# A two-layer 5x5 convolution: row combinations in unused columns, on ScalarE with adding transfers, and reflections on GpSimd

## The chip, the cores and the metric

The kernel runs on one core of a Trainium2 chip. The metric is the device time of one execution in microseconds (us). The kernel before takes 1879.63 us, the median of three runs (1878.62 to 1879.75).

## The reference

The input x has 8 images of 32 channels and 252x252 points, in float32. Two layers follow each other, and both compute the same thing with weights of their own:

```python
    # --- layer 0 (conv_preact) ---
    x = x + _L0_conv_ref(_gn(x), L0_conv_weight)
    # --- layer 1 (conv_preact) ---
    x = x + _L1_conv_ref(_gn(x), L1_conv_weight)
```

`_gn` is a group norm without scale and shift: 16 groups of 2 channels, with mean and variance over a group's whole image. The convolution is 5x5, 32 channels to 32, with two reflected points at each border; the reference writes it with Fourier transforms.

## The kernel before

**Layout.** An image is split by the parity of its columns and rows into four phases of 126x126. With 32 channels each, the phases fill the 128 partitions, and the 5x5 convolution becomes a 3x3 one from 128 to 128 channels. A *chunk* (b, l, c) is the piece c of 8 of image b in layer l (0 or 1); it has 16 rows of each phase, in 4 groups of 4.

**Arithmetic.** Rows are done by a short-convolution scheme with six points: six combinations of input rows, times six weight matrices, give four output rows. The combinations are built by VectorE (DVE) from two intermediates: `v` (16 rows: a row plus or minus the row two above it, `row_pairs`, L567 and L583) and `u` (2 times 4 rows: four times one row plus or minus the row two below it, `row_quads` and `last_rows`, L576, L577, L584). `point2` (L592) and `point1` (L602) are made from `u`; `point4` (L596), `point3` (L599) and `points05` (L609) from `v`. Along a row there are three taps, hence three matmuls for each point, accumulated in PSUM. For the two outer points many chunks are done "by columns" instead: DVE makes sums and differences along the row (`columns`, L618 to L628), and TensorE (PE) does 8 products of half the width (L707) instead of 6 full ones; four of these 8 read `sdiff` and go into the PSUM tile `extra`, and between the first two and the last two of them ScalarE (ACT) must halve a result (`seed_columns`, L711). The norm is folded into weights and biases, and the residual is added into the weights.

**Layer 1's v by transfers.** For nearly every chunk of layer 1, `v` isn't made by DVE: `row_sums` copies the rows of y by a transfer from GpSimd's queue (L557) into a tile with one buffer, and two adding transfers (L559, L560) add the rows two further down. L557 waits for the last reader of the tile's previous content (L609), L559 for the landing of L557.

**Buffers.** x's chunks lie in `xs`, 16 rows of 256 columns, in two buffers. A layer-0 chunk reads the even columns (0:256:2) alone. Most chunks are loaded once (`once`): partitions 0 to 63 get their image columns at odd and even places, `borders` (GpSimd, L148 to L154) makes the reflected columns, and `even_columns` (ACT, L159) copies the odd columns of partitions 0 to 63 into the even ones of partitions 64 to 127. In the tile pool `vpool` the names `v`, `va` and `u12` have one buffer each. Layer 0's results y stay in SBUF; `reflect` (ACT, L869 to L872) makes their four border columns, and rows in the first and last chunk.

**Order of the work.** The order is written out by hand. Every step is put in a table with a due time by `at`; the table is sorted by due time, and each engine executes its instructions in that order. After the first eight chunks, layer-0 chunks of image b+1 alternate with layer-1 chunks of image b. `begin(i)` is the planned start of the i-th chunk's matmuls. With two chunks by columns a layer-0 and a layer-1 chunk together take 27.2 in planned time, which is called a *pair* here. Around a layer-0 chunk planned at 0 and the layer-1 chunk at 13.6, ACT's order is: outer results of layer 0 (L785) at 0.05, seeds of PSUM (L729, L731) at 2.6 and 5.1, evacuations (L737, L744), `reflect` 7.8, `seed_columns` 9.3, small `even_columns` 9.35, the statistics of the next image (L235, L241) 9.8, squares (L860) 12.2, outer results of layer 1 (L785, or L773 where it isn't done by columns) at 13.65, interleaving for the output (L925), the seeds of the layer-1 chunk (L729, L731) at 16.2 and 18.7, its `seed_columns` 22.9. GpSimd's order is: small `borders` 5.5, `row_sums` L557 at 15.05, large `borders` 17.6, L559 and L560 at 22.0. SyncE's queue carries the loads of x (L143), the pieces for the statistics (L254) and the stores (L910).

Of the kernel before, what the change touches and what calls it, by code (L numbers as in the profile page):

```python
# [42 lines left out]
F32 = mybir.dt.float32  # L43
BF16 = mybir.dt.bfloat16
AF = mybir.ActivationFunctionType
ALU = mybir.AluOpType
# [3 lines left out]
P = 128  # L50
# [6 lines left out]
def tile_conv_preact_x2(ctx: ExitStack, tc: tile.TileContext, x: bass.AP, w0: bass.AP, w1: bass.AP, out: bass.AP):  # L57
# [34 lines left out]
    def at(t: float, fn, *args, **kw):  # L92
        table.append((t, len(table), fn, args, kw))
# [67 lines left out]
    def once(b: int, c: int) -> bool:  # L161

        return c != NCH - 1 and (c != 1 if b > 1 else c != 3 if b else True)

    def copied_late(b: int, c: int) -> bool:

        return once(b, c) and (b > 1 or (b == 1 and c > 3))

    def parts(b: int, c: int):

        if once(b, c):
            return ((0, 10), (10, 6)) if (b, c) == (0, 0) else ((0, 2), (2, 14))
        return ((0, ROWS),) + (((ROWS, 2),) if c == NCH - 1 else ())
# [363 lines left out]
    def transform(t0: float, t1: float, b: int, l: int, c: int, free: float = -100.0, now=(0, 0, 0)):  # L537

        wi = WIN[l]
        got = {}  # L540
        sent = l == 1 and (b, c) != (0, 0)

        def source():
            if l == 0:
                nxt = xs[b, c + 1] if c + 1 < NCH else xtail[b]
                return xs[b, c][:, :, 0:256:2], nxt[:, :, 0:256:2]
            return ytile[b, c], ytile[b, c + 1] if c + 1 < NCH else ytail[b]

        def row_sums(add: bool):

            t, nxt = source()
            if not add:

                i = max(order.index((b, l, c)) - order.index((B - 2, 1, NCH - 2)), 0)
                got["v"] = vpool.tile([P, ROWS, wi], F32, tag=("va", "v")[i % 2], name=f"v_{b}_{l}_{c}")
                got["vt"] = got["v"].rearrange("p (t i) w -> p t i w", i=4)
                G.dma_start(got["v"], t)  # L557
            else:
                G.dma_start(got["v"][:, 0 : ROWS - 2], t[:, 2:ROWS], accum_op=ALU.add)  # L559
                G.dma_start(got["v"][:, ROWS - 2 : ROWS], nxt[:, 0:2], accum_op=ALU.add)  # L560

        def row_pairs(j0: int = 0, j1: int = NT):
            if j0 == 0:
                got["v"] = vpool.tile([P, ROWS, wi], F32, tag="v", name=f"v_{b}_{l}_{c}")
            v, (t, nxt) = got["v"], source()
            r0, r1 = 4 * j0, min(4 * j1, ROWS - 2)
            (V.tensor_add if l else V.tensor_sub)(v[:, r0:r1], t[:, r0 + 2 : r1 + 2], t[:, r0:r1])  # L567
            got["vt"] = v.rearrange("p (t i) w -> p t i w", i=4)

        def row_quads(j0: int = 0, j1: int = NT):  # L570
            if j0 == 0:
                got["u"] = vpool.tile([P, 2, NT, wi], F32, tag="u12", name=f"u12_{b}_{l}_{c}")
            u1, u2, (t, nxt) = got["u"][:, 0], got["u"][:, 1], source()
            r0, k1 = 4 * j0, min(j1, NT - 1)
            f = 4.0 if l else -4.0
            stt(u1[:, j0:j1], t[:, r0 + 1 : 4 * j1 : 4], f, t[:, r0 + 3 : 4 * j1 : 4], ALU.mult, ALU.add)  # L576
            stt(u2[:, j0:k1], t[:, r0 + 2 : 4 * k1 : 4], f, t[:, r0 + 4 : 4 * k1 + 1 : 4], ALU.mult, ALU.add)  # L577

        def last_rows():

            u2, (t, nxt) = got["u"][:, 1], source()
            if not sent:
                (V.tensor_add if l else V.tensor_sub)(got["v"][:, ROWS - 2 : ROWS], nxt[:, 0:2], t[:, ROWS - 2 : ROWS])  # L583
            stt(u2[:, NT - 1], t[:, ROWS - 2], 4.0 if l else -4.0, nxt[:, 0], ALU.mult, ALU.add)  # L584

        def point2(j0: int = 0, j1: int = NT):
            if j0 == 0:
                t = tpool.tile([P, 2, NT, wi], F32, tag="t24", bufs=1, name=f"t24_{b}_{l}_{c}")
                if not fixed:
                    fixed.append(vpool.tile([P, 2, NT, WMAX], F32, tag="t13", name="t13"))  # L590
                ts[b, l, c] = {0: t, 1: fixed[0][:, :, :, 0:wi]}
            V.tensor_sub(ts[b, l, c][0][:, 0, j0:j1], got["u"][:, 1, j0:j1], got["u"][:, 0, j0:j1])  # L592

        def point4(j0: int = 0, j1: int = NT):
            vt = got["vt"][:, j0:j1]
            stt(ts[b, l, c][0][:, 1, j0:j1], vt[:, :, 1], -2.0, vt[:, :, 2], ALU.mult, ALU.add)  # L596

        def point3():
            stt(ts[b, l, c][1][:, 1], got["vt"][:, :, 1], 2.0, got["vt"][:, :, 2], ALU.mult, ALU.add)  # L599

        def point1():
            stt(ts[b, l, c][1][:, 0], got["u"][:, 1], norm[b, l][1][:, 1:2], got["u"][:, 0], ALU.add, ALU.add)  # L602

        def points05():
            if by_columns(b, l, c):
                t = vpool.tile([P, NT, 2, wi], F32, tag="u12", name=f"t05_{b}_{l}_{c}")
            else:
                t = tpool.tile([P, NT, 2, wi], F32, tag="t05", name=f"t05_{b}_{l}_{c}")
            stt(t, got["vt"][:, :, 0:2], 4.0 if l else -4.0, got["vt"][:, :, 2:4], ALU.mult, ALU.add)  # L609
            ts[b, l, c][2] = t  # L610

        def columns():

            t, (m, mo) = ts[b, l, c][2], evens_odds(l)
            sd = vpool.tile([P, 2, NT, 2, m], F32, tag="sdiff", name=f"sdiff_{b}_{l}_{c}")
            d = tpool.tile([P, NT, 2, 2, m], F32, tag="t05", name=f"d05_{b}_{l}_{c}")
            odd, even = t[:, :, :, 1 : 2 * m : 2], t[:, :, :, 2 : 2 * m + 1 : 2]
            V.tensor_add(sd[:, 0], odd, even)  # L618
            V.tensor_sub(sd[:, 1], even, odd)
            if m == mo:  # L620
                f = "p t e (m a) -> p (t e) a m"
                V.tensor_sub(
                    d.rearrange("p t e a m -> p (t e) a m"),
                    t[:, :, :, 0 : 2 * m].rearrange(f, a=2), t[:, :, :, 2 : 2 * m + 2].rearrange(f, a=2),
                )
            else:
                V.tensor_sub(d[:, :, :, 0], t[:, :, :, 0 : 2 * m : 2], t[:, :, :, 2 : 2 * m + 1 : 2])
                V.tensor_sub(d[:, :, :, 1, 0:mo], odd[:, :, :, 0:mo], t[:, :, :, 3 : 2 * mo + 2 : 2])  # L628
            ts[b, l, c][2] = d, sd

        if (b, l, c) == order[0]:
            at(t0 - 33.3, row_quads, 0, 2)
            at(t0 - 31, point2, 0, 2)
            for fn in (row_pairs, point4):
                at(t0, fn, 0, 2)
            at(t0 + 0.2, row_quads, 2, 4)
            at(t0 + 0.2, row_pairs, 2, 4)
            at(t0 + 0.2, last_rows)
            at(t0 + 0.2, point2, 2, 4)
            at(t0 + 0.2, point4, 2, 4)  # L640
            at(t0 + 4.9, point1)
            at(t0 + 5.5, point3)
            at(t0 + 6.2, points05)
        else:
            if sent:
                two = begin(order.index((b, l, c)) - 2)
                at(two + 1.45, row_sums, False)
                at(two + 8.4, row_sums, True)
            else:
                at(t0, row_pairs)  # L650
            for dt, fn in ((2, row_quads), (3.2, last_rows), (3.6, point2)):
                at(t0 + dt, fn)
            at(max(t0 + 4.2, free + 9.45) if sent else t0 + 4.2, point4)
            at(max(t0 + 5.5, free + 7.8), point1)
            at(max(t0 + 5.6, free + (11.1 if by_columns(*now) else 10.25)), point3)
            at(t1, points05)
            if by_columns(b, l, c):
                at(t1 + 1.5, columns)
# [184 lines left out]
    def keep(t1: float, t2, b: int, c: int, got):  # L843
# [17 lines left out]

        def reflect():
            lo, hi = (1 if c == 0 else 0), (ROWS - 1 if c == NCH - 1 else ROWS)
            y, copy, r = got["y"], A.copy, slice(lo, hi)

            def negated(dst, src):
                A.activation(dst, src, AF.Copy, scale=-1.0)
# [109 lines left out]
    def begin(i: int) -> float:  # L977

        return sum(10.2 + (own + [0.0])[j] + (late[j - 1] if j else 0.0) for j in range(i))
# [56 lines left out]
    for i, (b, l, c) in enumerate(order):  # L1036
# [11 lines left out]
        if i + 1 < len(order):  # L1048
# [3 lines left out]
            if nl == 0 and 2 < k < len(inputs):  # L1052
                kb, kc = inputs[k]
                for part in parts(kb, kc):
                    if copied_late(kb, kc):
                        at(t0 + 9.5, load, kb, kc, *part)
                        at(begin(i + 2) + 4.0 if part[0] else t1 + 5.5, borders, kb, kc, *part)
                        at(begin(i + 3) + 4.0 if part[0] else t1 + 9.35, even_columns, kb, kc, *part)
                        continue
# [77 lines left out]
```

## Time and profile before

| | before |
|---|---|
| median of 3 runs | 1879.63 us |
| the profiled execution: its own time | 1879.27 us |
| its span, first to last instruction | 1877.5 us |
| granted TensorE clock, mean | 0.994 |
| 16 DMA engines' busy share, 400 to 1600 us | 0.81 |
| packets, bytes on GpSimd's DMA queue | 27600, 134.20 MB (29.3% of the 16 engines' span) |
| packets, bytes on SyncE's DMA queue | 178832, 230.73 MB (49.8%) |

Busy times are sums over the span of one profiled execution; the program's own time is 1.8 us longer than the span. A row of instructions gives count, busy time and mean duration; a row of waits gives the total, the count and the longest wait in us.

### The profile page before, as it was taken

The numbers are of one execution on the slowest core, as the hardware profiler recorded it, in microseconds if no ns is written. First come the engines' busy times: TensorE is split into PE (matmuls) and PEld (weight loads), VectorE is DVE, ScalarE is ACT, GpSimd is POOL, SyncE is SP. The second block draws the span as 40 slices with busy tenths as digits, with TensorE's granted clock in tenths as the row PEclk, the third lists the DMA queues.
The fourth block names the chain that finished last, engine by engine and source line by source line (L and its number), as shares of the span: only waits on it lengthen the run. The fifth ranks groups of instructions, "written<-read, shape, count | busy, mean of one in ns | idle before, by whom it ended". The sixth has DMA issues, their size and how long they took to land.

```text
span 1877.5 us, 20381 instructions
## 1 busy us (share of the span) xinstructions
PE 1839.2 (98%) x5194; PEld 966.0 (51%) x5194; DVE 1731.2 (92%) x3030; ACT 1493.8 (80%) x2781; POOL 396.2 (21%) x855
## 2 busy tenths in 40 slices
PE   5999999999999999999999999999999999999998
PEld 4444455545555555555555455554555555555455
DVE  7988799999999999999999899999999999997796
ACT  5886788878887888888898798987898876765575
POOL 4543111131112211122111311113111141110211
PEclk8999999999999999999999999999999999999999
DMA  9877578878888877987878967888878866775785
GB/s 275 203 179 180 151 209 199 210 194 202 217 202 219 194 209 192 221 223 173 220 193 206 235 175 205 205 204 204 212 202 198 214 165 140 179 174 148 195 212 125
DMA packets 207110, 369.07 MB, mean 197 GB/s; under 512 B 19088, under 2 KB 173968, under 8 KB 196752
## 3 DMA queue, kind: packets, MB, share of 16 engines
q1 hardware_dynamic: 178832, 230.73, 49.8%
q0 software_dynamic: 27600, 134.20, 29.3%
q10 hardware_dynamic: 560, 2.83, 0.4%
q8 instruction: 41, 0.67, 0.2%
q14 instruction: 77, 0.63, 0.1%
HBM read 167.15 MB, written 67.39 MB: 125 GB/s over the span
## 4 chain that ended last, share of the span: by engine, by line
PE 80%; DVE 7%; DMA 6%; ACT 3%; issue 3%; SPq 0%; POOL 0%; DVEq 0%; ACTq 0%; POOLq 0%
PE m L685 28%; PE pairs L685 28%; PE sums L707 7%; PE extra L707 6%; PE sums L685 6%; PE extra L685 4%; DMA v<-y 2%; DMA st<-in_x_dram 1%; DMA v<-ytail 1%; DMA xs<-in_x_dram 1%; ACT o L925 1%; DVE sd L748 1%; DVE t L609 1%; DMA wraw<-in_L_conv_weight_dram 1%; DMA out_dram<-o 0%
## 5 line engine op out<-in xcount | busy, mean ns | idle before, releaser
L685 PE MATMUL pairs<-t,u 128*128 128x504 f32 (+2 forms) x1548 | 692.9, 586 | 5.4 <-ACT pairs L729 3.3
L685 PE MATMUL m<-t,u 128*128 128x508 f32 (+3 forms) x1560 | 674.8, 581 | 3.4 <-DVE u L526 1.9
L685 PEld LDWEIGHTS m<-t,u 128*128 128x128 f32 x1560 | 294.2, 189 | 317.1 <-issue 297.0
L685 PEld LDWEIGHTS pairs<-t,u 128*128 128x128 f32 x1548 | 290.2, 189 | 320.1 <-issue 289.1
L925 ACT COPY o<-y 64x508 f32<-64x508 f32 x496 | 327.5, 660 | 8.6
L748 DVE SCALAR_TENSOR_TENSOR sd<-sd,pairs 128x504 f32<-128x504 f32 (+2 forms) x258 | 164.2, 671 | 19.5 <-PE pairs L685 15.2
L707 PEld LDWEIGHTS extra<-sdiff,wc 128*128 128x128 f32 x680 | 125.9, 189 | 98.1 <-issue 47.8
L707 PE MATMUL extra<-sdiff,wc 128*128 128x252 f32 (+3 forms) x680 | 173.0, 376 | 3.4 <-ACT extra L711 2.3
L860 ACT ACTIVATE junk<-y,negk 128x1008 bf16<-128x1008 f32 (+1 forms) x144 | 147.4, 1024 | 31.1 <-PE extra L707 14.5
L557 POOL DMA_DIRECT2D v<-y x63 | 35.7, 567 | 622.7 <-DVE t L609 608.4
L737 ACT COPY sd<-m 128x504 f32<-128x504 f32 (+2 forms) x258 | 136.9, 581 | 33.3 <-DVE sums L794 28.1
L609 DVE SCALAR_TENSOR_TENSOR t<-v 128x1024 f32<-128x1024 f32 (+1 forms) x128 | 157.7, 1232 | 5.4 <-PE sums L685 5.4
L707 PE MATMUL sums<-d,u 128*128 128x252 f32 (+3 forms) x680 | 157.4, 374 | 0.0
L707 PEld LDWEIGHTS sums<-d,u 128*128 128x128 f32 x680 | 127.6, 189 | 24.9 <-issue 9.0
L685 PE MATMUL sums<-t,u 128*128 128x508 f32 (+5 forms) x312 | 133.6, 577 | 0.0
L567 DVE TENSOR_TENSOR v<-xs 128x1792 f32<-128x1792 f32 (+1 forms) x65 | 130.2, 2003 | 1.2
L241 ACT ACTIVATE st<-st,negk 128x1134 f32<-128x1134 f32 x98 | 121.7, 1242 | 3.2
L559 POOL DMA_DIRECT2D v<-y x63 | 54.3, 862 | 329.1 <-DMA v<-y 329.1
L159 ACT COPY xs<-xs 64x1792 f32<-64x1792 f32 (+2 forms) x97 | 109.3, 1129 | 13.4 <-POOL xs L151 11.1
L729 ACT ACTIVATE pairs<-m,means 128x504 f32<-128x504 f32 (+1 forms) x129 | 84.2, 653 | 44.5 <-PE m L685 36.0
L785 ACT ACTIVATE y<-sums 128x504 f32<-128x504 f32 (+1 forms) x158 | 94.5, 634 | 28.3 <-PE sums L707 19.2
L235 ACT ACTIVATE st<-st 128x1134 f32<-128x1134 f32 x98 | 112.5, 1148 | 5.0 <-DMA st<-in_x_dram 3.2
(174 smaller groups left out, 2529.7 us busy)
## 6 DMA issues: line engine op xcount, KB each, us to landing
v<-y POOLq DMA_DIRECT2D x63, 1032.0 KB, 6.1
st<-in_x_dram SPq DMA_DIRECT2D x111, 567.0 KB, 6.1
out_dram<-o SPq DMA_DIRECT2D x480, 126.0 KB, 5.9
v<-y POOLq DMA_DIRECT2D x63, 903.0 KB, 7.7
xs<-in_x_dram SPq DMA_DIRECT2D x96, 441.0 KB, 8.4
xs<-in_x_dram SPq DMA_DIRECT2D x44, 504.0 KB, 12.0
u<-ud SPq DMA_DIRECT2D x15, 1152.0 KB, 6.0
xs<-in_x_dram SPq DMA_DIRECT2D x16, 472.5 KB, 9.3
```

The source lines that it names most:

```text
L159: copy(t[64:128, :, 0:256:2], t[0:64, :, 1:256:2])
L235: A.activation(junk, src, AF.Identity, accum_out=acc[:, 0, i : i + 1])
L241: A.activation(junk, src, AF.Square, bias=negk, accum_out=acc[:, 1, i : i + 1])
L567: (V.tensor_add if l else V.tensor_sub)(v[:, r0:r1], t[:, r0 + 2 : r1 + 2], t[:, r0:r1])
L609: stt(t, got["vt"][:, :, 0:2], 4.0 if l else -4.0, got["vt"][:, :, 2:4], ALU.mult, ALU.add)
L685: T.matmul(dst, u[:, k, 2 - i, :], rhs[:, j0 + i0 : j0 + i1, i : i + wo], start=(i == 0 and not add), stop=(i == 2), skip_group_check=add,)
L707: T.matmul(dst[:, 0, use], w, rhs[:, use], start=(i == 2), stop=True, skip_group_check=(i != 2))
L737: A.copy(got["sd"][:, 1 + e], m24[e][:, 0:n])
L748: stt(d, d, -2.0, pairs13[e][:, 0:n], ALU.mult, ALU.add)
L785: A.activation(y, src, AF.Copy, scale=1.0 - 2 * i, **total(3 * i))
L860: A.activation(dst, src, AF.Square, bias=negk, scale=1.0 if i else -1.0, accum_out=acc[:, 1, at_ : at_ + 1])
L925: copy(got["o", h][halves[s], 0:m, cp::2], got["y"][halves[cp], r : r + m, :])
```

## The change

Layer 0's v is written into the odd columns of its own `xs` buffer, for images 2 to 7 and for chunks 4 to 7 of image 1. That keeps the buffer in use until `points05` has read v, so for the chunks that take such a buffer over (`deferred`) the load, the borders and the even columns get later due times, and all of them are loaded in two parts, of 2 and 14 rows.

For the layer-1 chunks behind chunk (0, 4) that follow a layer-0 chunk in the order (`sent_u`, 50 of them), `row_quads` and `last_rows` leave DVE. ACT writes four times the two inner rows of each group into the tile `v` (`four_times`), and three adding transfers from GpSimd's queue add the outer rows (`outer_rows`).

In chunks 1 to 6 `reflect` copies by GpSimd instead of ACT.

```diff
+    def among_columns(b: int, c: int) -> bool:
+        return b > 1 or (b == 1 and c > 3)
+    def deferred(b: int, c: int) -> bool:
+        i = inputs.index((b, c))
+        return i > 1 and among_columns(*inputs[i - 2])
     def parts(b: int, c: int):
+        if deferred(b, c):
+            return ((0, 2), (2, 14)) + (((ROWS, 2),) if c == NCH - 1 else ())
...
+        sent_u = l == 1 and (b, c) > (0, 4) and order[order.index((b, l, c)) - 1][1] == 0
...
+        def four_times():
+            got["u"] = vpool.tile([P, 2, NT, wi], F32, tag="v", name=f"ua_{b}_{l}_{c}")
+            src = source()[0].rearrange("p (t i) w -> p i t w", i=4)
+            A.activation(got["u"], src[:, 1:3], AF.Copy, scale=4.0)
+        def outer_rows():
+            t, nxt = source()
+            u1, u2 = got["u"][:, 0], got["u"][:, 1]
+            G.dma_start(u1, t[:, 3:ROWS:4], accum_op=ALU.add)
+            G.dma_start(u2[:, 0 : NT - 1], t[:, 4:ROWS:4], accum_op=ALU.add)
+            G.dma_start(u2[:, NT - 1], nxt[:, 0], accum_op=ALU.add)
         def row_pairs(j0: int = 0, j1: int = NT):
-            if j0 == 0:
+            if l == 0 and among_columns(b, c):
+                got["v"] = xs[b, c][:, :, 1:256:2]
+            elif j0 == 0:
                 got["v"] = vpool.tile([P, ROWS, wi], F32, tag="v", name=f"v_{b}_{l}_{c}")
...
                 at(two + 8.4, row_sums, True)
+                if sent_u:
+                    at(begin(order.index((b, l, c)) - 3) + 13.0, four_times)
+                    at(two + 1.4, outer_rows)
             else:
                 at(t0, row_pairs)
-            for dt, fn in ((2, row_quads), (3.2, last_rows), (3.6, point2)):
-                at(t0 + dt, fn)
+            for dt, fn in ((2, row_quads), (3.2, last_rows)):
+                if not sent_u:
+                    at(t0 + dt, fn)
+            at(t0 + 3.6, point2)
...
-            y, copy, r = got["y"], A.copy, slice(lo, hi)
+            y, copy, r = got["y"], A.copy if c in (0, NCH - 1) else G.tensor_copy, slice(lo, hi)
...
+                    if deferred(kb, kc):
+                        at(t1 + 6.0, load, kb, kc, *part)
+                        at(begin(i + 2) + 10.0 if part[0] else t1 + 11.0, borders, kb, kc, *part)
+                        if once(kb, kc):
+                            at(begin(i + 3) + 4.0 if part[0] else t1 + 12.6, even_columns, kb, kc, *part)
+                        continue
```

In the planned time of a pair (as above) the new places are: on ACT, `reflect` gone from 7.8 in chunks 1 to 6, small `even_columns` from 9.35 to 12.6, `four_times` at 13.0; on GpSimd, `reflect` at 7.8, small `borders` 11.0, `outer_rows` at 15.0 ahead of L557 at 15.05, large `borders` 23.6, behind L559 and L560; on SyncE's queue the load of x at 6.0, which before stood at 23.1 of the pair before.

## The prediction

> **What bounds the kernel now.** I read the engines' busy times first, then PE's waits, then one pair of chunks in order of time. The page's first part and the stretch from 400 to 1600 us (PE, weight loads, DVE, ACT, POOL, clock, DMA share):
>
> ```profile
> PE 1839.2 (98%) x5194; PEld 966.0 (51%) x5194; DVE 1731.2 (92%) x3030; ACT 1493.8 (80%) x2781; POOL 396.2 (21%) x855
> ...
> 400.00:1600.00 1200.00, 1198.10 (x3383) 630.16 (x3382) 1150.95 (x1978) 1011.54 (x1896) 230.30 (x502) 1.00 0.81 200
> ```
>
> TensorE (PE) idles 1.9 us in these 1200; the other 36 lie at the start, around 180 to 200 us and at the end, where the change touches little. The change removes no matmul, so it can hardly gain: what is left is the few waits of PE on its helpers.
>
> ```profile
> PE extra L707 <- ACT extra L711: 2.3, 8, 0.8
> PE extra L707 <- DVE sdiff L619: 0.5, 2, 0.3
> ```
>
> The danger is the reverse: an engine beside PE that gets late. In the pair at 1128 to 1155 us, ACT runs without a pause from L711 of the layer-0 chunk to L711 of the layer-1 chunk (start, duration):
>
> ```profile
> 1137.44 0.57 ACT L711 ACTIVATE extra<-extra 128x504 f32<-128x504 f32 x1 [0.37 <-PE extra L707]
> ...
> 1142.13 1.15 ACT L785 ACTIVATE y<-sums 128x512 f32<-128x512 f32 x2
> 1143.32 1.34 ACT L925 COPY o<-y 64x508 f32<-64x508 f32 x2
> 1144.68 0.66 ACT L729 ACTIVATE pairs<-m,means 128x508 f32<-128x508 f32 x1
> 1145.36 1.33 ACT L925 COPY o<-y 64x508 f32<-64x508 f32 x2
> 1146.81 0.57 ACT L731 COPY pairs<-m 128x508 f32<-128x508 f32 x1
> ...
> 1151.54 0.58 ACT L711 ACTIVATE extra<-extra 128x512 f32<-128x512 f32 x1
> ```
>
> PE's view of the same time:
>
> ```profile
> 1146.61 3.57 PE L685 MATMUL pairs<-t,u 128*128 128x508 f32 x8
> ...
> 1152.58 1.02 PE L707 MATMUL extra<-sdiff,wc 128*128 128x256 f32 x4
> ```
>
> L729 ends at 1145.34, 1.27 us before PE needs it (1146.61). L711 ends at 1152.12, 0.46 us before PE's second `extra` group.
>
> [...]L235's 1134 elements take 1148 ns[...].[...] L148's 64x4 copy taking 0.18 us at one place and 1.00 us at another[...].
>
> **The change part by part.**
>
> *Row combinations of layer 1.* DVE loses L576 (698 ns), L577 (557) and L584 (290): 1.55 us for each of 50 chunks, 77 us in all. DVE isn't the bound, so the worth is slack: DVE-made waits of PE vanish (0.5 us), and ACT's waits for DVE before L737 (28.1 us, 32 times) shrink, which shortens a few of ACT's late L711. Bounds 0 to -4 us; I take -2.
>
> ACT gains `four_times`, 1032 elements: [...]by the trace's L235 scaled 1.04[...]. It stands just ahead of L785 or L773 of the layer-1 chunk two places earlier. Where that is L773, ACT waits there for PE (70.9 us, 24 times, 3 us each) and swallows it: chunks 1, 5 and 7. Where it is L785 nothing absorbs it. L729 would end at 1146.3, still 0.3 early; L731 would start at 1147.8 instead of 1146.81, where it had waited for PE; L711 would end at 1153.0 to 1153.1, PE needing it at 1152.58 less some 0.05: **0.55 us late**. This holds where two by-columns chunks of layer 1 follow each other, chunks 2 and 3 of five images (image 6 has no statistics beside it): 10 x 0.55 = 5.5. At the change of image L729 has only 0.2 to 0.3 us of slack in the trace before some chunks (seeds at about 1089 and 1102 us): 0.4 an image, 2 in all. Together **+7.5 us**.
>
> The two places of ACT's small copy (L159, 0.43 us) lie in the same unbroken run, so moving it costs nothing; if the run had a gap between them, 0.43.
>
> *Reflections.* ACT loses 4 copies of 0.22 to 0.23 us in 48 chunks: 43 us. But they stand before L711 of layer 0, which waits for PE anyway (0.37 us in the row above); without them it waits 1.3. In an engine that runs in order the saving can't be carried behind that wait: 0 on PE's path. GpSimd gains 192 copies, 0.18 us (L148's shortest, as above) to 1 us[...], in stretches where it waits 6 to 13 us: 0.[...]
>
> *Adding transfers.* The rows are 516 bytes, so u takes 1024 packets. The trace's packet records have medians of 104 ns for an adding packet of 1032 bytes and 565 ns for 7224, a line that gives 66 ns at 516: 1024 x 66 / 16 = 4.2 us of all engines, against 0.19 x 27.2 = 5.2 us that a pair leaves free. It fits, but barely, by this count (which counts packets twice when two queues overlap). GpSimd must issue three more transfers: 0.55 us each by L557 (128 packets) if that doesn't grow with packets, up to 4.4 us for all if it does. They go ahead of L557, whose chain is this (GpSimd, then the reader of v on DVE):
>
> ```profile
> 1144.27 0.56 POOL L557 DMA_DIRECT2D v<-y  x1 [13.02 <-DVE t L609]
> ...
> 1151.27 0.87 POOL L559 DMA_DIRECT2D v<-y  x1 [5.93 <-DMA v<-y]
> 1151.82 1.23 POOL L560 DMA_DIRECT2D v<-y  x1
> ```
>
> `four_times` would end at about 1143.2, 1 us before L557 starts, so L557's data move 4.2 - 0.8 = 3.4 to 5.1 us later; elsewhere 1.4 to 4. v, landed at 1151.82 + 8.5 = 1160.3, is read at 1166.20 (L596), some 1164.7 with DVE's saving. So it mostly fits; where v is late already (L596 waits 17.6 us in 7 places), x's load, which no longer lies beside L559, gives about as much back. Bounds -1 to +10; I take +1.
>
> *v in x's columns.* DVE writes it at a stride of two. L793 does that already, at 675 ns against 688 for L792; reading at a stride costs nothing either (L576: 695 from xs, 698 from y). 0.
>
> *The later loads.* x is held until L609, about 3 us into the layer-0 chunk, and loaded at 6.0; the transfers land after 8 to 12 us (12.0 for the 504 KB ones). The small part (31.5 KB, 2.7 us) is wanted at 11, the large at 23.6. SyncE gains some 52 small issues of about 1 us, in a queue with gaps of several us: 0. The large `borders` now stand behind L559 and L560 and so behind the wait for L557's landing; ACT's L159 behind it has 5 to 10 us after L559 before. Less 2 us for issue and copies, less the 1.4 to 5.1 us from above, it keeps -0.5 to 2.6 us, and L731 behind it has 1.8 more: 0, bound +5.
>
> **Sum.** -2 + 7.5 + 1 + 0 = +6.5 on the profiled 1879.27 (span 1877.5 and 1.8 around it): 1885.8. That execution lies 0.4 us under the median of 1879.63. I forecast **1886**, +0.34%.
>
> **Rivals.** (0.2% is 3.8 us, about what a measurement of this kernel can tell from no change.)
>
> (a) *ACT late for L711*, as summed: 1882 to 1892, likeliest 1886. Chance 0.47.
>
> (b) *Absorbed*: not slower. ACT's insertion is paid by DVE's slack: L737 stops waiting for the sums (0.9 us a time), so L711 is ready where it was late before, and PE's waits on `extra` fall as the new ones come. It decides if the insertion costs under 0.5 us on the run from L711 to L711, the slack measured above; then the new stalls are 0 and the gains of 2 us stay: 1878 to 1881. For: the slack is 0.46, the insertion only twice that. Against: that run has no gap. Chance 0.30.
>
> (c) *Transfers late*: `outer_rows` holds GpSimd and the queue, L557 lands late, DVE waits at L596 and ACT at L159. It decides when L557 moves over 5 us. Then 1 us for each of 30 to 50 chunks, and more with full DMA engines: 1893 to 1930, centre 1905. Against: 4.2 us of packets and the slack shown. Chance 0.18.
>
> (d) *Faster*: DVE's slack removes most of PE's small waits and nothing new comes: 1874, about all that PE's rate between 200 and 1700 us leaves. Chance 0.05.
>
> Faster by over 0.2%: (d), 0.05. Within: (b) and a little of (a), 0.32. Slower: 0.63. The range leaves out about half of (c) and most of (d): 1877 to 1902.
>
> **What would show it.** PE's waits for L711 should rise from 2.3 us to about 8, at the layer-1 chunks 2 and 3; DVE's busy time fall by about 77, ACT's rise by about 8 (50 x 1.04 less 43); the new rows of `outer_rows` show the issue time, L559's wait for L557 should grow from 329 us, and L596's wait stay under 40. I am wrong if PE waits on DVE's L596 or L592, if L159 waits long for GpSimd, or if L711's waits don't grow.

## The result, and the profile after

| | before | after |
|---|---|---|
| median of the runs | 1879.69 us (4 runs) | 1946.74 us (1944.1 to 1949.28, 4 runs) |
| ratio, 95% interval | | 1.0359 [1.0343, 1.0376] |
| span of the profiled execution | 1877.5 us | 1943.6 us |
| granted TensorE clock, mean | 0.994 | 0.984 |

The kernel is 67 us slower, ten times the forecast of 6.5 us and outside the range of 1877 to 1902. Lines of the kernel after are up to 33 higher than before: L557, L559 and L560 became L570, L572 and L573; L596 became L624, L711 became L744, L731 became L764, L757 became L790. New are L579 (`four_times`) and L584 to L586 (`outer_rows`).

The page's first part and the stretch from 400 to 1600 us, as shown of before:

```profile
PE 1862.6 (96%) x5194; PEld 971.7 (50%) x5194; DVE 1662.2 (86%) x2880; ACT 1508.3 (78%) x2639; POOL 630.1 (32%) x1236
...
400.00:1600.00 1200.00, 1160.96 (x3229) 605.45 (x3228) 1039.79 (x1771) 988.31 (x1734) 390.89 (x763) 0.99 0.96 212
```

DVE lost 69 us of work and the DMA engines' share rose from 0.81 to 0.96, both close to what was expected. But PE, idle for 1.9 us of the 1200 before, is idle for 39. Its waits (total, times, longest in us):

```profile
PE extra L740 <- DVE sdiff L647: 21.9, 17, 3.1
PE pairs L718 <- ACT pairs L764: 18.9, 8, 2.8
...
PE extra L740 <- ACT extra L744: 6.1, 16, 0.8
PE m L357 <- DVE mv L347: 4.1, 6, 0.9
```

The third row is the wait that was predicted (8 us, 6.1 came). The first two are larger and longer. Most of their time comes in pairs, one of each a few us apart, at seven places of the program, five of them where the last layer-1 chunk of an image meets the next image. The trace of that place at the end of layer 1 of image 1, engine by engine. GpSimd (start, duration; in brackets the idle time before):

```profile
622.08 1.31 POOL L584 DMA_DIRECT2D ua<-y  x1
622.89 1.80 POOL L585 DMA_DIRECT2D ua<-y  x1
623.64 1.96 POOL L586 DMA_DIRECT2D ua<-y  x1
624.99 1.18 POOL L570 DMA_DIRECT2D v<-y  x1
...
637.73 0.85 POOL L572 DMA_DIRECT2D v<-y  x1 [11.56 <-DMA v<-y]
638.28 1.17 POOL L573 DMA_DIRECT2D v<-y  x1
```

DVE:

```profile
636.85 1.27 DVE L781 SCALAR_TENSOR_TENSOR sd<-sd,pairs 128x508 f32<-128x508 f32 x2
644.26 0.69 DVE L790 SCALAR_TENSOR_TENSOR y<-pairs,sd 128x508 f32<-128x508 f32 x1 [6.15 <-issue]
...
647.20 0.68 DVE L796 TENSOR_TENSOR sd<-pairs,sd 128x508 f32<-128x508 f32 x1
```

ACT and PE:

```profile
647.96 0.56 ACT L764 COPY pairs<-m 128x504 f32<-128x504 f32 x1 [5.75 <-DVE sd L796]
...
648.58 1.11 PE L718 MATMUL pairs<-t,u 128*128 128x504 f32 x2 [2.84 <-ACT pairs L764]
651.84 1.00 PE L740 MATMUL extra<-sdiff,wc 128*128 128x189 f32 x2 [2.15 <-DVE sdiff L647]
```

Read it from PE backwards. PE waits for a seed of ACT, which waits for DVE's last reading of `pairs` (L796), which stands behind L790. L790 writes the result y of chunk (1, 1, 7), and it stood still for 6.15 us with all its inputs there. The profile gives "issue", which means that it shows nothing that L790 waited for; but the last packet of 7224 bytes of L572, the addition for chunk (2, 1, 0), ends at 643.84, and L790 starts at 644.26. That suggests that DVE waits for transfers that *read* something that L790 is about to *write*.

What they share is a buffer. All y tiles, of both layers, come from one pool of nine (`ypool`, tag "y"), and which free buffer a new y gets is fixed when the program is built. The built program lists the addresses:

```
new y of chunk    before: address, last held by      after: address, last held by
(1, 1, 6)         115168   (1, 1, 5)                 123424   (1, 1, 5)
(2, 0, 7)          73888   (1, 0, 7)                  73888   (1, 0, 7)
(1, 1, 7)         115168   (1, 1, 6)                  82144   (2, 0, 0)
(3, 0, 0)         123424   (2, 0, 0)                 123424   (1, 1, 6)
```

Before, layer 1's y passes one buffer on to itself up to chunk (6, 1, 5), because at these places no other is free: y (2, 0, 0) is still to be read by DVE (`row_quads` of chunk (2, 1, 0)). After, `row_quads` is gone; the last readers of y (2, 0, 0) are the transfers L584 to L586, L570, L572 and L573, which in the program stand *ahead* of L790. By the program's order the buffer is free, and the new y is put there; in time, the transfers are still reading. I call this a borrowed buffer. Counted over the program, before has none and after has nine: the transfers stand 43 to 57 instructions ahead of the new y there, and 90 or more wherever else they were a buffer's last readers. Six are the y of the last chunks (b, 1, 7) of images 0 to 5, the others (0, 1, 5), (6, 1, 1) and (7, 0, 6). The waits of L790 are nine as well, and the kernel before has none at this step (L757):

```profile
DVE y L790 <- issue: 30.9, 6, 6.1
...
DVE y L790 <- DMA v<-y: 15.8, 3, 8.6
```

PE has the same 5194 instructions in the same order in both kernels, so their starts can be compared one by one. Within 18 us of these nine waits PE falls back by 52.0 us, of 68.5 us over the whole program.

### The profile page after: what moved, and what is told of

It is laid out like the page before. It is cut to its first block, busy times and chain, and to the rows that moved or that the text cites. A ratio compares the mean times of both kernels' runs of the same rounds, so it can differ in the third digit from the quotient of the medians.

```text
span 1943.6 us, 20804 instructions
## 1 busy us (share of the span) xinstructions
PE 1862.6 (96%) x5194; PEld 971.7 (50%) x5194; DVE 1662.2 (86%) x2880; ACT 1508.3 (78%) x2639; POOL 630.1 (32%) x1236
## 3 DMA queue, kind: packets, MB, share of 16 engines
q0 software_dynamic: 81200, 160.63, 40.1%
## 4 chain that ended last, share of the span: by engine, by line
PE 50%; DMA 17%; DVE 13%; ACT 9%; issue 7%; POOL 3%; SPq 1%; ACTq 0%; DVEq 0%; POOLq 0%
PE pairs L718 19%; PE m L718 17%; DMA v<-y 11%; PE extra L740 5%; PE sums L740 4%; PE sums L718 4%; DMA xs<-in_x_dram 3%; PE extra L718 2%; DMA out_dram<-o 2%; ACT o L958 2%; DMA st<-in_x_dram 1%; ACT junk L893 1%; ACT st L246 1%; DVE sd L781 1%; ACT ua L579 1%
## 5 line engine op out<-in xcount | busy, mean ns | idle before, releaser
L718 PE MATMUL pairs<-t,u 128*128 128x504 f32 (+2 forms) x1548 | 704.2, 593 | 22.4 <-ACT pairs L764 18.9
L740 PE MATMUL extra<-sdiff,wc 128*128 128x252 f32 (+3 forms) x680 | 181.8, 391 | 28.3 <-DVE sdiff L647 21.9
L572 POOL DMA_DIRECT2D v<-y x63 | 53.5, 849 | 464.5 <-DMA v<-y 446.1
L740 PEld LDWEIGHTS extra<-sdiff,wc 128*128 128x128 f32 x680 | 129.6, 196 | 132.0 <-issue 52.0
L148 POOL COPY xs<-xs 64x4 f32<-64x4 f32 (+3 forms) x126 | 70.3, 558 | 349.4 <-DMA xs<-in_x_dram 294.5
L770 ACT COPY sd<-m 128x504 f32<-128x504 f32 (+2 forms) x258 | 136.9, 581 | 46.4 <-DVE sums L827 40.8
L740 PE MATMUL sums<-d,u 128*128 128x252 f32 (+3 forms) x680 | 157.3, 373 | 0.0
L740 PEld LDWEIGHTS sums<-d,u 128*128 128x128 f32 x680 | 127.5, 189 | 25.2 <-issue 7.8
L764 ACT COPY pairs<-m 128x504 f32<-128x504 f32 (+1 forms) x129 | 73.3, 568 | 82.1 <-PE m L718 41.0
L584 POOL DMA_DIRECT2D ua<-y x50 | 64.7, 1295 | 195.7 <-ACT ua L579 195.5
L790 DVE SCALAR_TENSOR_TENSOR y<-pairs,sd 128x504 f32<-128x504 f32 (+1 forms) x129 | 87.0, 674 | 46.8 <-issue 30.9
L159 ACT COPY xs<-xs 64x1792 f32<-64x1792 f32 (+2 forms) x97 | 109.3, 1129 | 22.8 <-POOL xs L151 20.4
L570 POOL DMA_DIRECT2D v<-y x63 | 80.1, 1271 | 114.9 <-DVE t L637 88.7
```

The costliest lines, as they stand in the source:

```text
L159: copy(t[64:128, :, 0:256:2], t[0:64, :, 1:256:2])
L718: T.matmul(dst, u[:, k, 2 - i, :], rhs[:, j0 + i0 : j0 + i1, i : i + wo], start=(i == 0 and not add), stop=(i == 2), skip_group_check=add,)
L740: T.matmul(dst[:, 0, use], w, rhs[:, use], start=(i == 2), stop=True, skip_group_check=(i != 2))
L764: A.copy(dst, src)
L770: A.copy(got["sd"][:, 1 + e], m24[e][:, 0:n])
L790: stt(yrow(2), s1, 4.0 * f, s0, ALU.mult, op, **total(2))
```

## The experiments

A ratio is to the kernel before, run beside the experiment, with a 95% interval. The *copy-to-addition time* is the time from the start of GpSimd's copy of v (L557, L570 after) to the start of the addition behind it (L559, L572 after).

Three theories stood at first. *Queue*: u's packets make v's copy late, and all else follows. *Load*: the later loads of x crowd the DMA engines. *ScalarE*: the ScalarE step is to blame. The account above, *buffer*, came out of the second run below; the two runs with an own buffer test it.

**Without u.**

```diff
-        sent_u = l == 1 and (b, c) > (0, 4) and order[order.index((b, l, c)) - 1][1] == 0
+        sent_u = False
```

> The changed kernel with layer 2's row combinations u back on DVE (neither the ScalarE step nor the three adding transfers); v in the columns of x's buffer, the later loads and GpSimd's reflections stay. Queue theory (u's 1024 packets stand ahead of v's copy in GpSimd's DMA queue; copy, row addition and with it the release of layer 1's y buffer come late, and DVE waits ahead of the y step): the copy-to-addition time falls from 9.3 back to about 6.4 us, DVE's waits ahead of the y step go, 1880 us (1874 to 1888). Load theory (the later loads of x fill the DMA engines while v is copied): the loads are still late, 1915 to 1945 us. ScalarE theory (the ScalarE step makes the seeds late): 1880 us as well; told apart from the queue theory by the run with the ScalarE step alone.

("Layer 2" in this text is layer 1 of the document, counted from one, and "layer 1's y" is layer 0's.)

1875.23 us, ratio 0.9979 [0.9972, 0.9986]: **a little faster than the kernel before**, by 3.6 us or 0.2%. The loads lie where the change put them, so the load theory is out as a cause by itself. What has changed beside the kernel before is seen in DVE's waits. Before:

```profile
DVE t L596 <- DMA v<-y: 17.6, 7, 3.5
...
DVE t L596 <- DMA v<-ytail: 7.2, 4, 2.8
```

Without u:

```profile
DVE t L624 <- DMA v<-y: 0.2, 1, 0.2
```

The line (L624 there) waits once for a transfer: the median copy-to-addition time is 6.2 us against 6.4, and L624 has its v in time. How much of the 3.6 us comes by this way isn't shown: PE's idle time falls by only 1.5 us in the profiled executions (38.3 and 36.8).

**u behind the copy.**

```diff
-                    at(two + 1.4, outer_rows)
+                    at(two + 1.46, outer_rows)
```

> The changed kernel with the three adding transfers of u issued behind v's copy instead of ahead of it; same transfers, same bytes, same ScalarE step. Queue theory: the copy starts and lands about 3 us earlier in most chunks and up to 6 us earlier at the change of image, 1885 to 1900 us. Load theory and ScalarE theory: nothing that they blame has moved, 1935 to 1948 us.

2028.78 us, ratio 1.0807 [1.0769, 1.0845]: 82 us *slower* than the changed kernel. All theories were wrong here. The copy did come earlier (median copy-to-addition 6.7 us instead of 9.3), so the queue theory in its plain form fell: the transfers it wanted earlier were earlier, and the time grew. This run led to the addresses: its program has 25 borrowed buffers instead of nine, and DVE waits 25 times:

```profile
DVE y L790 <- DMA v<-y: 100.9, 19, 9.1
...
DVE y L790 <- issue: 25.0, 6, 5.0
```

**No u in the first chunks.**

```diff
+        sent_u = ... and c > 0
```

> The changed kernel with u on DVE in the first chunk of each image alone (6 of 50 chunks), adding transfers elsewhere. Queue theory, with the loss at the change of image (6 stalls of 6 to 8 us): 1946 less 40 to 50, so 1897 to 1907 us. If the delay is the same in every chunk and only shows where there is least slack, the stall moves to the next chunk: 1925 to 1946 us. Load theory: 1940 us or more.

1907.78 us, 1.0152 [1.0136, 1.0168], 39 us less than the changed kernel, from 6 of 50 chunks. The queue theory said nearly so (1897 to 1907), but its delay is still there: the median copy-to-addition time is 9.2 us. The buffer theory explains both: with `row_quads` back on DVE in chunk (b, 1, 0), y (b, 0, 0) is no longer free too early; three borrowed buffers are left, and L790 waits three times (15.3 us).

**The ScalarE step alone.**

```diff
-        sent_u = ...
+        sent_u = False
-                if sent_u:
+                if (b, c) > (0, 4) and order[order.index((b, l, c)) - 1][1] == 0:
                     at(begin(order.index((b, l, c)) - 3) + 13.0, four_times)
-                    at(two + 1.4, outer_rows)
```

> As the run without u, but ScalarE still writes four times the rows into a buffer that nothing reads (u itself is computed by DVE): the ScalarE part of the change without its transfers. Queue theory: the run without u plus the 4 to 8 us that the prediction gave the late seeds, 1880 to 1892 us. ScalarE theory: near the changed kernel, 1925 to 1946 us.

1888.41 us, 1.0051 [1.0033, 1.0069]. Against the run without u it is 13.2 us by the medians and 9.7 by the profiled spans (1885.1 and 1875.4), where 7.5 was predicted; the profiled execution here has the least of four times (1886.84), that of the run without u the greatest of 19 (1877.14). PE's waits in this run (its lines lie one lower: L739 for L740, L743 for L744), and one of the run without u:

```profile
PE m L357 <- DVE mv L347: 4.7, 6, 0.9
...
PE extra L739 <- ACT extra L743: 3.0, 15, 0.2
```

```profile
PE extra L740 <- ACT extra L744: 1.5, 7, 0.2
```

With PE's starts compared one by one, as above, the late `extra` is there where the prediction had it: at the layer-1 chunks 2 and 3 of five images PE falls back ten times, by 0.3 to 0.4 us (0.55 predicted), 3.5 us in all. What the prediction did not have is the first row: once for each of six images PE stops for the mean of a layer's statistics, 4.9 us in all. DVE computes the mean behind a step (L795) that waits for ACT's outer results (L817); at the second of the six these end 1 us later than without u (591.7 and 590.7), while PE is only 0.1 us later. The kernel before has this wait once (0.7 us, L346 there), the run without u not at all.

**An own buffer for layer 1's y.** All of the change stays; one of the nine buffers is kept for layer 1's y up to chunk (6, 1, 5), as the kernel before has it in effect.

```diff
+    own_y = {}
...
-            got["y"] = ypool.tile(...)
+            got["y"] = own_y.get(l == 1 and (b, c) < (B - 2, NCH - 2))
+            if got["y"] is None:
+                got["y"] = ypool.tile(...)
+                if l == 1 and (b, c) < (B - 2, NCH - 2):
+                    own_y[True] = got["y"]
```

> The changed kernel, all transfers, steps and due times as they are, but layer 1's second-convolution y keeps one buffer of its own up to chunk (6, 5), as it has in the kernel before, so that it is never given the buffer of a layer 1 input that u's and v's transfers are still reading. Buffer theory (nearly all the loss is DVE waiting ahead of the y step for a buffer that the transfers still read, at 8 places): 1946 less about 51, 1888 to 1900 us; the copy-to-addition time stays at about 9.3 us and costs nothing. Queue theory (the late copy costs by itself): the wait moves to the reader of v on DVE, 1920 to 1946 us.

1893.38 us, 1.0075 [1.0048, 1.0102]: 53.4 us of the 67 are gone, with the same transfers at the same due times, where the buffer theory expected about 51 and the queue theory under 26. The addition is as late as in the changed kernel (GpSimd waits 448.2 us for the copy here, 446.1 in the changed kernel). One borrowed buffer is left, with a wait of 0.6 us. DVE now waits at the reader of v (L624, here L625):

```profile
DVE t L625 <- issue: 41.0, 11, 5.2
DVE t L625 <- DMA v<-y: 24.9, 11, 4.7
```

Of these 66 us of waiting on DVE little reaches PE, whose waits on `extra` and the mean are small; the second row is that of the run with the ScalarE step alone:

```profile
PE extra L741 <- ACT extra L745: 6.0, 16, 0.8
PE m L357 <- DVE mv L347: 4.6, 6, 0.9
PE extra L741 <- DVE sdiff L648: 4.1, 9, 0.8
```

So a late v is nearly harmless, as the prediction had it (this run is 5.0 us over the one with the ScalarE step alone); a late *release* of y was not.

**Own buffer, u behind the copy.** Both edits above together.

> The run with u's transfers behind v's copy (2029 us), with the own y buffer. Buffer theory: its 25 borrowed y buffers were its whole loss, so 1883 to 1898 us, level with or a little under the run with u ahead of the copy and an own buffer. If u's transfers behind the copy are bad in themselves (they delay v's row addition and u's reader), it stays over 1930 us.

1907.33 us, 1.0148 [1.0126, 1.017]. Of the 150 us that u behind the copy had lost, 121 are gone with the borrowed buffers: the main part of the expectation holds. Its figure doesn't: it is 14 us over the run with u ahead. DVE's wait for v is nearly gone (L625: 5.9 us, against 66), so the late v isn't the reason. Here x's small load lands late, the small `borders` wait for it (GpSimd waits 343.0 us for x's loads at L148, 303.5 with u ahead), and ACT's copy of the columns behind them is late before its seeds:

```profile
ACT xs L159 <- POOL xs L151: 32.7, 16, 4.4
```

```profile
PE pairs L719 <- ACT pairs L763: 20.1, 12, 3.0
```

(17.9 and 3.5 us in the run with u ahead.) That u's packets delay x's load fits the places in the trace; it was not tested apart.

**The reflections on ScalarE, without u.**

```diff
-            y, copy, r = got["y"], A.copy if c in (0, NCH - 1) else G.tensor_copy, slice(lo, hi)
+            y, copy, r = got["y"], A.copy, slice(lo, hi)
```

> The run without u (1875.2 us), with the reflections back on ScalarE: v in the columns and the later loads alone. Prediction's step (the reflections are worth nothing): 1874 to 1877 us. If the reflections' leaving ScalarE is what made the run without u faster than the kernel before: 1878 to 1880 us.

1875.76 us, 0.9982 [0.9975, 0.9989], level with 1875.23. The reflections are worth nothing; the 3.6 us come from v in x's columns and the later loads together, which were not told apart.

**Four times the rows by GpSimd, own buffer.**

```diff
-            A.activation(got["u"], src[:, 1:3], AF.Copy, scale=4.0)
+            G.tensor_scalar(got["u"], src[:, 1:3], 4.0, None, ALU.mult)
```

> The run with the own y buffer, with four times the rows computed by GpSimd instead of ScalarE. ScalarE alone cost 13 us (1888.4 against 1875.2): if that is ScalarE's time in front of the seeds, this run is 8 to 14 us under the run with the own buffer and ScalarE. If GpSimd's work stands in front of the transfers that it issues and makes them late enough to count, it is level or slower.

1886.83 us, 1.0052 [1.0029, 1.0075], 6.5 us below the run with ScalarE, but the two intervals overlap, and their profiled spans are equal (1892.8 and 1892.7). Inconclusive; the profiled execution has the greatest of six times (1894.68; the least is 1883.57). In it the wait for the mean at L357 is 1.3 us instead of 4.6, and L159 waits 35.8 us for GpSimd instead of 17.9.

## Why the prediction was wrong

The sign was right, for a small part of the reason. The sum was -2 + 7.5 + 1 + 0 = +6.5. The runs give, each term as a difference of two medians (from three sessions, in which the kernel before took 1879.69, 1878.83 and 1879.15 us):

| term | predicted | measured |
|---|---|---|
| v in columns, later loads, reflections | 0 | -3.6 (without u, less before) |
| `four_times` on ACT | +7.5 | +13.2 (ScalarE step alone, less without u) |
| DVE's relief and the adding transfers | -2 + 1 | +5.0 (own buffer, less ScalarE step alone; the intervals overlap) |
| borrowed y buffers | not in the sum | +53.4 (changed, less own buffer) |

**The step that failed** is that on the row combinations: "DVE isn't the bound, so the worth is slack". It took DVE's three instructions as 1.55 us of time and nothing else. They were also the last *readers* of y in the program's order, and so they held its buffer until after the transfers had landed. Taking them away handed the buffer out earlier while it was read later. The prediction followed the one buffer of v, and its readers L557 and L596; it never asked who holds the nine of y. Moving a reader off an engine raises that question. What the runs showed in place of "slack" is 53.4 us, the loss that goes when layer 1's y keeps a buffer of its own.

**The transfers' time** was mis-sized, too. Its parts were good: u's packets have a median of 67 ns (66 estimated), by which they take 4.3 us of all engines a chunk (4.6 by their sum), and the DMA share rose by 0.15, which is 4.2 / 27.2. But 4.2 us counts u's own packets alone. For chunk (2, 1, 0) these add up to 4.3 us of all engines, yet they ran from 626.71 to 634.26, 7.5 us, beside SyncE's packets, which took 40.1% of all engines' time in that stretch. How the engines divide their time between the queues was not shown. v's copy, which comes later in the same queue, was issued at 624.99, and its first packet starts only at 631.98. Median copy-to-addition time rose from 6.4 to 9.3 us, and at the change of image from 7.0 to 12.7 (chunk (2, 1, 0)). The bound of +10 for this term was in the prediction; it covers what v's readers lost (5.0 us for this term with the own buffer), not what y's buffer did.

**Rival (c)**, transfers late, came nearest, with 1893 to 1930. It had the right cause of lateness, and the wrong victim: L596 and L159. L624 did wait more, 56.6 us against 24.8, where "under 40" was said:

```profile
DVE t L624 <- issue: 29.8, 10, 4.8
DVE t L624 <- DMA v<-y: 26.8, 10, 4.6
```

But the run with the own buffer has 66 us of these waits and is only 5.0 us over the one with the ScalarE step alone.

**ScalarE.** The mechanism was right, and its size nearly: by PE's starts, the step alone costs 3.5 us at the ten places named (5.5 predicted) and 0.3 us at each of five changes of image (0.4 predicted). The step itself took 1063 ns by the trace (L579, mean of 50), where L235 of the trace of before, scaled, gave 1.04 us. At 26 of the 50 places the outer results behind it (L818) start 0.09 us before it ends, so that it holds ACT for 0.97 us there. The prediction's places in time imply about as much (L731 at 1147.8 instead of 1146.81); the trace of before has such overlaps too: at 39 places L711 starts 0.10 us before the end of the L925 ahead of it. Missing was the statistics' mean, 4.9 us. That PE's waits for L744 come to 6.1 us in the changed kernel, near the 8 predicted, is in part luck: at chunk 3 they are 0.7 us there and 0.2 with the step alone, so something comes on top there with the transfers, which was not traced. ACT's waits for DVE, which were to shrink from 28.1 us (L737), are 40.8 in the changed kernel (L770) and 29.0 with the own buffer (L771): no relief is seen.

**The reflections** were worth nothing, as said. ACT's busy time falls by 32.3 us for them (1494.8 with them, 1462.5 without), not 43: in the trace of before the four copies of a chunk take 0.80 us together, where their durations add up to 0.89, and at 53 of 64 places the first (L869) starts 0.11 us before the end of the L744 ahead of it. On GpSimd the 192 copies took 0.20 to 3.05 us each (median 0.21, 17 of them over 1 us), where the prediction had 0.18 to 1; what makes some of them long, and whether they hold DVE up, was not shown. With `four_times` ACT's busy time rose by 14.5 us, not 8.

**v in x's columns** was written at no extra cost, as said: L595 takes 2020 ns at a stride of two (52 times) and 2046 into a tile of its own (11 times). (The 688 ns that the prediction has for L792 are those of L794; L792 takes 685 at that shape.)

**The later loads** cost nothing where u stays on DVE, as the run without u shows; that they would help v's copy was said only as "gives about as much back". Without u L596's 24.8 us of waits shrink to 0.2; the same run has v in x's columns too, so which of the two does it isn't shown. SyncE's issues of the small parts (63 KB) take 0.42 us in median in the changed kernel, where about 1 us was said.

**The stalls cost more than their waits.** At the place above PE waits 2.84 + 2.15 us, but the next chunk starts 8.4 us later than it should: by PE's starts, compared with the kernel before, PE is 16.8 us behind ahead of the place and 25.1 after it. The stretches 645 to 648 and 651 to 660 us (the columns as above):

```profile
645.00:648.00 3.00, 0.74 (x2) 0.00 (x0) 3.00 (x5) 0.04 (x1) 0.00 (x0) 1.00 0.00 0
...
651.00:654.00 3.00, 2.16 (x5) 1.81 (x6) 3.00 (x5) 2.91 (x11) 0.00 (x0) 0.52 1.09 176
654.00:657.00 3.00, 3.00 (x5) 1.18 (x4) 1.37 (x3) 2.91 (x6) 0.00 (x0) 0.50 0.01 2
657.00:660.00 3.00, 3.00 (x14) 2.63 (x13) 2.92 (x7) 2.14 (x5) 0.67 (x1) 0.84 0.48 160
```

After the pauses the granted clock is 0.50 for about 6.8 us (2.9 us of the second stretch, all of the third, 1 us of the fourth), and PE, busy for 6.1 us of them, loses the other 3 us there.

What stays open: by which rule a new tile gets one of several free buffers. With two free, the changed program took the one that transfers were still reading in nine places and the other one elsewhere; the edits changed the outcome without showing the rule. Nor is the +5.0 for DVE's relief and the transfers clear of the noise.

## What to carry to other kernels

When a step is moved from an engine to a transfer, list every tile that it read, and ask who is its last reader now, in the program's order and in time: the buffer comes free at the first, and the wait is paid at the second, on whichever engine writes the next tile into it (here on DVE, nine waits of L790, 46.7 us). Where tiles of different lives share one pool, an edit that moves no byte can change who gets which buffer (25 instead of nine bad ones for a due time moved by 0.06); a buffer of its own for the short-lived tile, one of the same nine, left one such buffer in both orders, at no cost in space. A kernel whose first engine is 98% busy has little to win from unloading the second: here the two versions without u, which leave DVE its work, are the fastest of all, at 0.998 of the kernel before.

## What the runs showed of the hardware

Two pauses of PE of 2.84 and 2.15 us, with 1.1 us of matmuls between them, were followed by some 6.8 us at a granted clock of 0.50 (651.2 to 657.9 us). How long a pause must be for that was not shown. No price of a stall in the prediction had this in it.

Three adding transfers of 516-byte rows occupy GpSimd for 1.3, 1.8 and 2.0 us by the profile, but start 0.76 us apart (medians); the copy behind them starts 2.1 to 5.3 us after the first. At its quickest the queue loses less by them than their rows add up to: in this trace issuing overlaps.
